# Gate and up by the Strassen identity over two levels, with token sums and h in DRAM

## The chip, the cores and the metric

The kernel runs on one core of one Trainium2 chip. The metric is the device time in microseconds of one execution. The profile gives the span from the first to the last instruction of one profiled execution, and the time of that execution beside it.

## What is computed

The input x is (8, 256, 1024) in fp32: 2048 tokens of 1024 features. Four layers follow, each added to its input, each with LoRA adapters of rank 16 that are picked for each of the eight batch entries by four index vectors.

```python
# L0: a linear layer with bias and LoRA, 1024 -> 1024
x = x + (einsum('bti,oi->bto', x, W) + b + ((x @ A[id]) @ B[id]) * 2)
# L1: a gated MLP, 1024 -> 2752 -> 1024, LoRA (scale 0.5) on gate, up and down
gate = lora_add(einsum('bnh,fh->bnf', x, W_gate), x, A_gate, B_gate)
up   = lora_add(einsum('bnh,fh->bnf', x, W_up),   x, A_up,   B_up)
act  = silu(gate) * up
x = x + lora_add(einsum('bnf,hf->bnh', act, W_down), act, A_down, B_down)
# L2, L3: LoRA alone
x = x + einsum('bnr,bor->bno', einsum('bni,bri->bnr', x, B2[id]), A2[id])
x = x + einsum('bnr,bor->bno', einsum('bni,bri->bnr', x, B3[id]), A3[id])
```

Everything stays in fp32.

## The kernel before

**Tiling.** On the chip x is transposed: features on the 128 partitions (8 chunks of 128, `NC`), tokens along the free dimension. The tokens are worked in two blocks (`NBLK`) of 1024, and each block is two halves (`NN`) of 512[...]. The hidden size 2752 is 21 chunks of 128 (`FC`) and a remainder of 64 (`FR`), in six groups: five of four chunks and one of the last chunk with the remainder.

**Products.** Every large product uses one level of the Strassen identity in Winograd's form, seven products for eight. The class `Job` writes one such product out: its weights as a 2 x 2 block matrix (two chunks of outputs by two halves of the inputs) against the tokens as a 2 x 2 block matrix (two halves of the inputs by two halves of the tokens). `weight_sums` (L244 to L247) makes the four sums of the weights on VectorE for each job, `token_sums` (L253 to L256) the four sums of the tokens once for each stage. `Job.run` fixes the order by hand: products 1, 5, 6, 3, then hooks (`middle`), then 7, 2, 4. `Job.block` (L274) issues one product: for gate and up four matmuls of 128x128 weights on 512 tokens, for down two (one in its last group). Products accumulate in the banks `pa`, `pb`, `pc`; ScalarE copies three intermediate states out (`early`, L328), VectorE adds (L306 and the adds in `done`).

**Gate and up.** One job is one chunk f: its output rows are gate chunk f and up chunk f, so 21 jobs a block (`gate_up`). After the products `lora` adds the LoRA parts with four matmuls of 32 rows (`expand`, L230), then `done` computes silu(gate) x up with ScalarE's sigmoid (L516) and VectorE. The remainder's 64 gate rows and 64 up rows are one ordinary product (`mixed`, L470, with L481 for its LoRA), and `shrink2` computes the LoRA inputs `tgu` through `shrink_into` (L206). x1 (the input of layer 1), its sums and h stay in SBUF, in a pool of 67 tiles of 128x512.

**Down.** When a group of gate and up is complete, `shrink_hidden` and `sum_hidden` run in the middle of the next group's first job, and four down jobs for that group follow. Their results add up in x2. The last group carries the remainder and down's LoRA as extra rows. `tables23`, `shrink23` and `last_layers` (L725) then do layers 2 and 3 and store the output.

**Order.** The list `jobs` is the order of all engines: block 0 with layer 0 (four jobs, the first one a `plain` product, L420, while x arrives), then `mixed`, then 21 gate-up jobs with the down jobs of group g - 1 after the first job of group g, then the last down jobs and `last_layers`; then block 1. SP's queue loads each job's weights one job ahead (`load_pair`, two times 512 KB; `following.loaded = following.load()`), and the following job's weight sums are issued before products 2 and 4 of this one. GpSimd only gathers LoRA tables (L176).

Of the kernel before, what the change touches and what calls it, by code (L numbers as in the profile page):

```python
# [7 lines left out]
F32 = mybir.dt.float32  # L8
# [10 lines left out]
R = 16  # L19
# [11 lines left out]
GROUPS = ((0, 4), (4, 8), (8, 12), (12, 16), (16, 20), (20, 21))  # L31


@with_exitstack
def kernel(
# [11 lines left out]
    wg: bass.AP,  # L47
    wu: bass.AP,
    wmix: bass.AP,
# [6 lines left out]
    bmix: bass.AP,  # L56
# [22 lines left out]

    nc = tc.nc  # L80

    const = ctx.enter_context(tc.tile_pool(name="const", bufs=1))
    xpool = ctx.enter_context(tc.tile_pool(name="x", bufs=67))
    wpool = ctx.enter_context(tc.tile_pool(name="w", bufs=5))
    swpool = ctx.enter_context(tc.tile_pool(name="sw", bufs=2))
    cpool = ctx.enter_context(tc.tile_pool(name="c", bufs=8))
# [4 lines left out]
    tpool = ctx.enter_context(tc.tile_pool(name="t", bufs=2))  # L91
    ps_a = ctx.enter_context(tc.tile_pool(name="ps_a", bufs=2, space=bass.MemoryType.PSUM))
    ps_b = ctx.enter_context(tc.tile_pool(name="ps_b", bufs=1, space=bass.MemoryType.PSUM))
    ps_c = ctx.enter_context(tc.tile_pool(name="ps_c", bufs=2, space=bass.MemoryType.PSUM))
    ps_l = ctx.enter_context(tc.tile_pool(name="ps_l", bufs=1, space=bass.MemoryType.PSUM))
    ps_t = ctx.enter_context(tc.tile_pool(name="ps_t", bufs=1, space=bass.MemoryType.PSUM))
    ps_d = ctx.enter_context(tc.tile_pool(name="ps_d", bufs=1, space=bass.MemoryType.PSUM))

    def xtile(name):
        return xpool.tile([P, 512], F32, tag="x", name=name)  # L100

    def ctile(name):
        return cpool.tile([P, 512], F32, tag="c", name=name)
# [38 lines left out]

    off_b = const.tile([P, 4, NBLK], I32, tag="off_b", name="off_b")
    off_gu = const.tile([P, NBLK], I32, tag="off_gu", name="off_gu")
    sel_v = sel.rearrange("p l (k n) -> p l k n", n=NN)
    for r in range(4):
        rows = slice(32 * r, 32 * r + 32)
        nc.vector.tensor_copy(off_b[rows], sel_v[rows, :, :, r // 2])
        nc.vector.tensor_copy(off_gu[rows], sel_v[rows, 1, :, r % 2])
    nc.vector.tensor_scalar(off_b, off_b, float(R), rank_f, op0=ALU.mult, op1=ALU.add)  # L150
    nc.vector.tensor_scalar(off_gu, off_gu, float(R), rank_f, op0=ALU.mult, op1=ALU.add)
    nc.vector.tensor_single_scalar(off_gu[64:], off_gu[64:], float(SLOTS1 * R), op=ALU.add)
# [19 lines left out]
    nc.scalar.dma_start(out=bias, in_=b0)  # L172

# [28 lines left out]
    def shrink_into(ps, r, a, chunks, c, n, src, start, stop):  # L202


        v = a.rearrange("p b (r c) -> p (b r) c", c=chunks)[:, 2 * n * R : 2 * (n + 1) * R, c]
        nc.tensor.matmul(ps[32 * r : 32 * r + 32, :], v, src, start=start, stop=stop)  # L206

    def shrink(a, src, scale, name):

        ps = ps_t.tile([P, 512], F32, tag="t", name=name)  # L210
        for c in range(HC):
            for r in range(4):
                k = (r % 2) * HC + c
                shrink_into(ps, r, a, NC, k, r // 2, src[k][r // 2], c == 0, c == HC - 1)
        return rank_out(ps, scale, f"{name}_s")

    def shrink2(a, b, src, scale, name):

        ps = ps_t.tile([P, 512], F32, tag="t", name=name)
        order = [0, 1, 2, 4, 5, 6, 3, 7]  # L220
        for c in order:
            for r in range(4):
                shrink_into(
                    ps, r, (a, b)[r // 2], NC, c, r % 2, src[c][r % 2], c == order[0], c == order[-1]
                )
        return rank_out(ps, scale, f"{name}_s")
# [11 lines left out]


    def weight_sums(a11, a12, a21, a22, width, name):  # L240

        s = swpool.tile([P, 3, 512], F32, tag="sw", name=name)
        s2, s3, s4 = (s[:, j, :width] for j in range(3))
        nc.vector.tensor_sub(s3, a11, a21)  # L244
        nc.vector.tensor_add(a21, a21, a22)
        nc.vector.tensor_sub(s2, a21, a11)
        nc.vector.tensor_sub(s4, a12, s2)  # L247
        return {1: a11, 2: a12, 3: s4, 4: a22, 5: a21, 6: s2, 7: s3}

    def token_sums(b11, b12, b21, b22, t1, name):  # L250

        t2, t3, t4 = (xtile(f"{name}_t{j}") for j in (2, 3, 4))
# [4 lines left out]
        return {1: b11, 2: b21, 3: b22, 4: t4, 5: t1, 6: t2, 7: t3}  # L257

    class Job:


        def __init__(self, name, load, sums, moving, lora, early, done):
            self.name, self.load, self.make, self.moving = name, load, sums, moving
            self.lora, self.early, self.done = lora, early, done
            self.before, self.middle, self.plain = [], [], None

        def sums(self):
            self.stationary = self.make(self.loaded)

        def block(self, ps, j, start=False):  # L270
            moving = self.moving()
            w = self.stationary[j]
            for k, m in enumerate(moving):
                nc.tensor.matmul(  # L274
                    ps,
                    w[:, k * P : (k + 1) * P],
                    m[j],
                    start=start and k == 0,
                    stop=k == len(moving) - 1,
                    skip_group_check=True,  # L280
                )

        def run(self, following):
            for hook in self.before:
                hook()
            if following:
                following.loaded = following.load()
            if self.plain:
                self.plain(self.loaded, lambda: [hook() for hook in self.middle])
                following.sums()  # L290
                return
            n = self.name
            pa = ps_a.tile([P, 512], F32, tag="a", name=f"pa_{n}")
            pc = ps_c.tile([P, 512], F32, tag="c", name=f"pc_{n}")
            s1, p5, s2 = (ctile(f"{j}_{n}") for j in ("s1", "p5", "s2"))
            self.block(pa, 1, start=True)
            self.early(1, s1, pa)
            self.block(pc, 5, start=True)
            self.early(5, p5, pc)
            self.block(pa, 6)  # L300
            self.early(6, s2, pa)
            self.block(pc, 3)
            for hook in self.middle:
                hook()
            self.block(pa, 7)
            nc.vector.tensor_add(p5, p5, pa)  # L306
            if following:
                following.sums()
            pb = ps_b.tile([P, 512], F32, tag="b", name=f"pb_{n}")
            self.block(pb, 2, start=True)  # L310
            self.block(pa, 4)
            pl = self.lora(pa, pb, pc) if self.lora else None
            self.done(s1, s2, p5, pa, pb, pc, pl)

    def by_halves(w):
        return [w[j][:, h : h + HC, :].rearrange("p c m -> p (c m)") for j in (0, 1) for h in (0, HC)]

    def load_pair(w, i, v, j, name):
        out = []
        for x, y in ((w, i), (v, j)):  # L320
            t = wpool.tile([P, NC, P], F32, tag="w", name=f"{name}_{len(out)}")
            nc.sync.dma_start(out=t, in_=x[y])
            out.append(t)
        return out

    def copy(dst, src, bias_=None):
        if bias_ is None:
            nc.scalar.activation(dst, src, AF.Identity)  # L328
        else:
            nc.scalar.activation(dst, src, AF.Identity, bias=bias_)  # L330

    jobs = []
    arrival = [c + h for c in range(HC) for h in (0, HC)]

    def block(blk):
        st = {}


        def load_x():
            st["x"] = xs = [[None] * NN for _ in range(NC)]  # L340
            for n in range(NN):
                for i, k in enumerate(arrival):
                    xs[k][n] = xtile(f"x_{blk}_{k}_{n}")
# [6 lines left out]
            st["xm"] = [  # L350
                token_sums(*xs[c], *xs[c + HC], xtile(f"x_{blk}_{c}_t1"), f"x_{blk}_{c}")
                for c in range(HC)
            ]

        st["x1"] = [[None] * NN for _ in range(NC)]
        st["x1m"] = [None] * HC

        def layer0(o):
            p = o + HC

            def early(j, dst, ps):
                b, x = {1: (o, (o, 0)), 5: (p, (p, 1)), 6: (o, (o, 1))}[j]
                copy(dst, ps, bias[:, b : b + 1])
                nc.vector.tensor_add(dst, dst, st["x"][x[0]][x[1]])

            def lora(pa, pb, pc):
                pl = ps_l.tile([P, 512], F32, tag="l", name=f"pl_0_{blk}_{o}")
                b, t = st["b0"], st["t0"]
                expand(pb, b, o, t, 0, 64)
                expand(pc, b, o, t, 64, 128)  # L370
                expand(pa, b, p, t, 0, 64)
                expand(pl, b, p, t, 64, 128, start=True)
                return pl
# [473 lines left out]
```

## Time and profile before

| what | value |
|---|---|
| median of 3 runs | 1947.23 us (1945.86 to 1947.27) |
| the profiled execution's own time | 1945.51 us |
| its span | 1943.7 us |
| granted TensorE clock | 0.999 |
| a gate-up job (starts at 170.28, 195.58, 220.88 us) | 25.30 us |
| VectorE add of two 128x512 tiles | 687 to 691 ns |
| ScalarE copy of a 128x512 bank (L328) | 597 ns |
| weight load of 512 KB, from issue to landing | 3.4 us |

In the profile PE is TensorE's matmuls, PEld its weight loads, DVE VectorE, ACT ScalarE, POOL GpSimd, SP the engine whose queue issues most transfers. A group row names line, engine, operation, destination and sources, the shapes and the number of records; then the busy time and the mean duration of one in ns, and the idle time of the engine just ahead of them with what ended it. A matmul record starts when the pass starts and its end is modelled, so records of neighbours overlap, and spacing is read from starts in the timeline.

### The profile page before, as it was taken

What the parts mean: (1) busy time and instruction counts of PE and PEld (TensorE: products, weight loads), DVE (VectorE), ACT (ScalarE), POOL (GpSimd) and SP (SyncE); (2) the same over time, 40 slices, a digit from 0 to 9 for tenths busy, and PEclk for the clock granted to TensorE, in tenths of its full rate; (3) what the DMA queues carried; (4) which work ended last, traced back from release to release, by engine and by line L of the source; (5) the groups of instructions that cost most, each with busy time, mean ns of one, the idle gap of its engine ahead of it and who ended that gap; (6) DMA issues with size and microseconds to landing.
All of it is one profiled execution on the core that took longest, in us unless ns stands there. A gap on an engine that the chain in (4) does not pass through costs nothing.

```text
span 1943.7 us, 13193 instructions
## 1 busy us (share of the span) xinstructions
PE 1925.8 (99%) x5140; PEld 820.6 (42%) x5140; DVE 809.9 (42%) x1370; ACT 263.1 (14%) x435; POOL 120.1 (6%) x137
## 2 busy tenths in 40 slices
PE   8999999999999999999999999999999999999998
PEld 3444444444444444444344444444444444444442
DVE  5332344254345236147734233432533442543466
ACT  0001111111111102012200011111111111111121
POOL 5001010010010010012110100000000100100000
PEclk9999999999999999999999999999999999999999
DMA  6111111111111111114231111111111101111102
GB/s 210 46 45 42 35 61 33 43 52 43 43 52 43 44 45 36 41 41 135 74 118 43 54 44 49 46 44 45 40 43 34 61 33 44 46 43 44 35 25 87
DMA packets 36622, 104.23 MB, mean 54 GB/s; under 512 B 6032, under 2 KB 7184, under 8 KB 36560
## 3 DMA queue, kind: packets, MB, share of 16 engines
q1 hardware_dynamic: 25216, 82.32, 13.1%
q0 software_dynamic: 4864, 10.56, 1.8%
q10 hardware_dynamic: 6480, 10.51, 1.6%
q8 instruction: 40, 0.66, 0.1%
q14 instruction: 22, 0.18, 0.0%
HBM read 94.98 MB, written 8.39 MB: 53 GB/s over the span
## 4 chain that ended last, share of the span: by engine, by line
PE 98%; DVE 1%; DMA 0%; issue 0%; ACT 0%; DVEq 0%; SPq 0%
PE pa L274 51%; PE pc L274 25%; PE pb L274 12%; PE pb L230 3%; PE pp L420 1%; PE pm L470 1%; PE td L206 1%; PE p L206 1%; PE tgu L206 1%; PE p L230 1%; DVE x L725 0%; PE t L206 0%; DMA x<-in_xT_dram 0%; PE pa L230 0%; PE pm L481 0%; DVE hr L579 0%
## 5 line engine op out<-in xcount | busy, mean ns | idle before, releaser
L274 PE MATMUL pa<-x_t,swgu 128*128 128x512 f32 x672 | 303.1, 594 | 0.0
L306 DVE TENSOR_TENSOR p<-p,pa 128x512 f32<-128x512 f32 x97 | 66.6, 687 | 522.0 <-PE pa L274 521.9
L274 PEld LDWEIGHTS pa<-x_t,swgu 128*128 128x128 f32 x672 | 126.9, 190 | 164.0 <-issue 164.0
L274 PE MATMUL pa<-h_t,swd 128*128 128x512 f32 x352 | 168.6, 597 | 0.0
L328 ACT ACTIVATE s<-pa 128x512 f32<-128x512 f32 x180 | 107.5, 597 | 385.8 <-PE pa L274 385.3
L274 PE MATMUL pa<-x,wgu 128*128 128x512 f32 x336 | 154.9, 603 | 0.0
L274 PE MATMUL pc<-x,swgu 128*128 128x512 f32 x336 | 151.1, 592 | 0.0
L274 PE MATMUL pc<-x_t,wgu 128*128 128x512 f32 x336 | 151.0, 592 | 0.0
L274 PE MATMUL pa<-x_t,wgu 128*128 128x512 f32 x336 | 151.0, 592 | 0.0
L274 PE MATMUL pb<-x,wgu 128*128 128x512 f32 x336 | 151.0, 592 | 0.0
L516 ACT ACTIVATE sg<-s 128x512 f32<-128x512 f32 x42 | 26.5, 630 | 659.5 <-DVE s L515 659.5
L274 PEld LDWEIGHTS pa<-h_t,swd 128*128 128x128 f32 x352 | 65.4, 190 | 87.8 <-issue 82.1
L274 PEld LDWEIGHTS pa<-x,wgu 128*128 128x128 f32 x336 | 61.0, 190 | 90.0 <-issue 90.0
L625 DVE TENSOR_TENSOR s<-s,x 128x512 f32<-128x512 f32 x96 | 66.3, 691 | 75.6 <-ACT s L328 75.4
L274 PEld LDWEIGHTS pa<-x_t,wgu 128*128 128x128 f32 x336 | 63.8, 190 | 80.4 <-issue 78.7
L274 PEld LDWEIGHTS pb<-x,wgu 128*128 128x128 f32 x336 | 63.8, 190 | 80.4 <-issue 80.4
L274 PEld LDWEIGHTS pc<-x,swgu 128*128 128x128 f32 x336 | 63.8, 190 | 80.4 <-issue 80.4
L274 PEld LDWEIGHTS pc<-x_t,wgu 128*128 128x128 f32 x336 | 63.8, 190 | 80.4 <-issue 80.4
L244 DVE TENSOR_TENSOR swgu<-wgu,wgu 128x512 f32<-128x512 f32 x42 | 28.9, 689 | 139.1 <-DMA wgu<-in_wu_dram 139.1
L274 PE MATMUL pa<-h,wd 128*128 128x512 f32 x176 | 84.4, 598 | 0.0
L274 PE MATMUL pc<-h,wd 128*128 128x512 f32 x176 | 83.4, 592 | 0.0
L176 POOL DMA_INDIRECT bgu<-in_bgu_dram,off_gu x12 | 11.4, 947 | 1105.3 <-PE pl L230 1104.7
(170 smaller groups left out, 2107.9 us busy)
## 6 DMA issues: line engine op xcount, KB each, us to landing
wgu<-in_wg_dram SPq DMA_DIRECT2D x42, 512.0 KB, 3.4
wgu<-in_wu_dram SPq DMA_DIRECT2D x42, 512.0 KB, 3.5
wd<-in_wd_dram SPq DMA_DIRECT2D x40, 512.0 KB, 3.4
w<-in_w_dram SPq DMA_DIRECT2D x16, 512.0 KB, 3.6
out_dram<-x ACTq DMA_DIRECT2D x32, 256.0 KB, 4.2
x<-in_xT_dram SPq DMA_DIRECT2D x24, 256.0 KB, 5.9
x<-in_xT_dram ACTq DMA_DIRECT2D x8, 256.0 KB, 6.4
wmix<-in_wmix_dram SPq DMA_DIRECT2D x2, 512.0 KB, 3.5
```

What stands on the lines that cost most here:

```text
L176: nc.gpsimd.indirect_dma_start(out=t, out_offset=None, in_=table, in_offset=bass.IndirectOffsetOnAxis(ap=off, axis=0),)
L206: nc.tensor.matmul(ps[32 * r : 32 * r + 32, :], v, src, start=start, stop=stop)
L230: nc.tensor.matmul(ps, b[lo:hi, i * P : (i + 1) * P], t[lo:hi, :], start=start, stop=True, skip_group_check=True,)
L244: nc.vector.tensor_sub(s3, a11, a21)
L274: nc.tensor.matmul(ps, w[:, k * P : (k + 1) * P], m[j], start=start and k == 0, stop=k == len(moving) - 1, skip_group_check=True,)
L306: nc.vector.tensor_add(p5, p5, pa)
L328: nc.scalar.activation(dst, src, AF.Identity)
L420: nc.tensor.matmul(pss[j, n], wt[:, c, :], x[c][n], start=i == 0, stop=i == NC - 1)
L470: nc.tensor.matmul(pss[n], w[:, c, :], x1[c][n], start=c == order[0], stop=c == order[-1], skip_group_check=True,)
L516: nc.scalar.activation(sg[0], s1, AF.Sigmoid)
L625: nc.vector.tensor_add(dst, dst, base(*{1: (o, 0), 5: (p, 1), 6: (o, 1)}[j]))
```

## The change

**Two levels.** For gate and up the outer level of the identity takes the weights as (gate, up) by (two halves of the inputs) and the tokens as (two halves of the inputs) by (two halves of the tokens). Each of its seven products is again split into seven. So 49 products stand where two full levels have 64, on quarters of 256 tokens. The class `Quads` does this for a group of four chunks (`nq` = 2, two pairs of chunks side by side in one bank). Its seven outer products are seven *units*, in the order 1, 2, 3, 5, 6, 7, 4; each unit runs seven blocks of `nq` x 2 matmuls of 128x128 weights on 256 tokens. The last block of a unit is put off to the middle of the next (`pending`, `flush`). X, E, Z, Y are four accumulators in SBUF; at the end of units 2, 6, 7, 4 one of them is a finished quarter of gate or up.

**Rest.** The last chunk, the remainder of 64 + 64 rows and the LoRA shrink (as 128 extra columns of the weights) make a group of their own with `nq` = 1 (`rest`), which runs first of a block's groups. It takes the place of `mixed`, `shrink2` and the tables `be` and `bm`.

**Weight sums.** `outer` and `inner_sums`, and the weight sums of down, are on GpSimd. Layer 0's stay on VectorE.

**Tokens.** The token sums of both levels are made once for each block, on VectorE, after layer 0 (`prepare_tokens`); layer 0 of both blocks now comes ahead of everything else. They are stored to DRAM (`toks`, 7 x 2 tiles of 128 x 1792), and each unit loads its two tiles of 917 KB (`load_tok`). x1 goes to DRAM (`x1d`) and is loaded for down as x2. h goes to DRAM for each group (`hd`), and down, which runs as a stage of its own after all groups of a block, loads it.

**Work beside.** `done` puts the finishing of a quarter (LoRA expand into a bank of its own, add, sigmoid, products, store, shrink for down) into the queue `beside`, from which each slot of a unit takes a share. SBUF is one pool of 22 tiles of 8 KB a partition; PSUM is 2 banks a, 1 b, 1 c and 4 l.

Layer 0's evictions add bias and x on VectorE straight from the bank; its order of outputs is 0, 2, 1, 3. A down eviction is one VectorE add into x2.

```diff
-    class Job:
-        def block(self, ps, j, start=False):
-            moving = self.moving()
-            w = self.stationary[j]
-            for k, m in enumerate(moving):
-                nc.tensor.matmul(ps, w[:, k * P : (k + 1) * P], m[j], ...)
...
-        first = gate_up(0, 0)
-        first.before.insert(0, mixed)
...
+    class Quads:
+            for s in range(len(ORDER)):
+                u = Unit(f"{name}_{s}", lambda at, s=s: self.step(s, at), share)
+                u.before(1, 0, lambda s=s: self.load_tok(s))
+                u.before(1, 1, lambda s=s: self.inner_sums(s))
+                self.units.append(u)
+            first = self.units[0]
+            first.before(3, 0, lambda: (self.load("B11"), self.load("B12")))
+            first.before(2, 0, lambda: self.load("B22"))
+            first.before(1, 0, lambda: self.load("B21"))
+            self.units[0].at(2, lambda: self.outer("T3", "B22", "B12", "sub"))
+            self.units[1].at(3, lambda: self.outer("B12", "B12", "B11", "sub"))
+            self.units[2].at(2, lambda: self.outer("B11", "T3", "B11", "add"))
+            self.units[4].at(2, lambda: self.outer("B21", "B21", "B11", "sub"))
...
+        def load_tok(self, s):
+            i = ORDER[s]
+            self.tok[i] = []
+            for kk in range(2):
+                t = big(f"tk_{self.name}_{s}_{kk}")[:, : 7 * S]
+                nc.sync.dma_start(out=t, in_=toks[self.blk][PLACE[i], kk])
+                self.tok[i].append(t)
...
+        def inner_sums(self, s):
...
+            nc.gpsimd.tensor_add(s1, m21, m22)
+            nc.gpsimd.tensor_sub(s2, s1, m11)
+            nc.gpsimd.tensor_sub(s3, m11, m21)
+            nc.gpsimd.tensor_sub(s4, m12, s2)
...
+            def block(ps, j, start=False):
+                for q in range(nq):
+                    for kk in range(2):
+                        nc.tensor.matmul(
+                            ps[:, q, :],
+                            w[j][:, q, kk * P : (kk + 1) * P],
+                            tok[kk][:, SLOT[j] * S : (SLOT[j] + 1) * S],
...
+            def first(r, k, ps):
+                if old is None:
+                    copy(view(out, r, k), ps)
+                else:
+                    nc.vector.tensor_add(view(out, r, k), view(old, r, k), ps)
+            def more(r, k, ps):
+                nc.vector.tensor_add(view(out, r, k), view(out, r, k), ps)
+                whole(r, k)
+            also = {5: ("Z", "Y"), 6: ("Z", "X"), 7: ("Y", "X")}.get(i)
+            def whole(r, k):
+                if also:
+                    a, b = (view(self.c[x], r, k) for x in also)
+                    nc.vector.tensor_add(a, a, b)
+            at(0)
+            pa = half(ps_a, "pa")
+            block(pa, 1, start=True)
+            first(0, 0, pa)
+            at(1)
+            pc = half(ps_c, "pc")
+            block(pc, 5, start=True)
+            first(1, 1, pc)
+            at(2)
+            flush()
+            at(3)
+            block(pa, 6)
+            first(0, 1, pa)
+            at(4)
+            block(pc, 3)
+            more(0, 1, pc)
+            at(5)
+            pb = half(ps_b, "pb")
+            block(pb, 2, start=True)
+            more(0, 0, pb)
+            at(6)
+            block(pa, 7)
+            more(1, 1, pa)
+            at(7)
+            def last():
+                block(pa, 4)
+                first(1, 0, pa)
+                whole(1, 0)
+                if i in self.ENDS:
+                    n, table, key = self.ENDS[i]
+                    self.done(n, table, self.c.pop(key))
+            pending.append(last)
...
+            def done(n, table, c):
+                beside.append((0, lora))
+                for r in range(4):
+                    beside.append(
+                        (0.69, lambda r=r: nc.vector.tensor_add(c[:, r], c[:, r], lo[r]))
+                    )
+                    if table == 0:
+                        beside.append(
+                            (0, lambda r=r: nc.scalar.activation(lo[r], c[:, r], AF.Sigmoid))
+                        )
...
+                if (n, 1 - table) in held:
+                    u, v = held[n, 1], held[n, 0]
+                    for r in range(4):
+                        beside.append(
+                            (0.69, lambda r=r: nc.vector.tensor_mul(u[:, r], u[:, r], v[:, r]))
+                        )
+                    def store():
+                        nc.sync.dma_start(out=hd[blk][g, n], in_=u.rearrange("p r t -> p (r t)"))
+                        shrink_hidden(g, n, [u[:, r] for r in range(4)])
+                    beside.append((0.7, store))
...
+        rest()
+        for g in range(REST):
+            job(g)
...
+    for blk in range(NBLK):
+        layer0(blk)
+    for blk in range(NBLK):
+        gate_up(blk)
+        down_projection(blk)
...
+        def at(slot):
+            for f in hooks.pop((i, slot), ()):
+                f()
+            spent = 0
+            while beside and spent < u.share:
+                cost, f = beside.popleft()
+                f()
+                spent += cost
```

In the prediction, lines of the changed kernel are L386 for the matmuls of `block`, L418 for the add of `first`, L421 for that of `more`, L774 for the store of h. X, Z, Y, E, `whole` and u x v (the product of up and silu(gate)) are as above. A block is one inner product of the identity: A7 is inner product 7, into the bank `pa`. pd is the shrink of h for down's LoRA, td the sum that collects it.

## The prediction

> **What bounds the kernel now.** I read the busy line and the chain of waits first, because they tell whether removed work can be seen in the end.
>
> ```profile
> PE 1925.8 (99%) x5140; PEld 820.6 (42%) x5140; DVE 809.9 (42%) x1370; ACT 263.1 (14%) x435; POOL 120.1 (6%) x137
> DMA packets 36622, 104.23 MB, mean 54 GB/s; under 512 B 6032, under 2 KB 7184, under 8 KB 36560
> q1 hardware_dynamic: 25216, 82.32, 13.1%
> PE 98%; DVE 1%; DMA 0%; issue 0%; ACT 0%; DVEq 0%; SPq 0%
> ```
>
> TensorE works 99% of the span and is 98% of the chain: every product left out is time, until something else is late. VectorE has 58% left, GpSimd 94%. q1 moved 82.32 MB in 13.1% of 1943.7 us, so 323 GB/s when it runs.
>
> The timeline of TensorE gives the price of a product:
>
> ```profile
> 416.82 3.60 PE L274 MATMUL pb<-x,wgu 128*128 128x512 f32 x8
> 420.25 3.60 PE L274 MATMUL pa<-x_t,wgu 128*128 128x512 f32 x8
> ...
> 424.85 1.98 PE L274 MATMUL pa<-h,wd 128*128 128x512 f32 x4
> 426.67 1.88 PE L274 MATMUL pc<-h,wd 128*128 128x512 f32 x4
> ```
>
> The last column counts records; one fp32 matmul of the program makes two (passes). Four matmuls start 3.43 us apart (420.25 - 416.82), so one costs 0.857 us, a pass 429 ns. The group rows say 594 ns because records overlap; I use starts. The weight loads have records of their own:
>
> ```profile
> 424.85 0.30 PEld L274 LDWEIGHTS pa<-h,wd 128*128 128x128 f32 x2 [0.76 <-issue]
> 425.39 0.19 PEld L274 LDWEIGHTS pa<-h,wd 128*128 128x128 f32 x1 [0.24 <-issue]
> 899.57 1.09 PEld L676 LDWEIGHTS pba<-bb,a2s 128*32 128x32 f32 x32 [0.76 <-issue]
> 899.57 1.21 PE L676 MATMUL pba<-bb,a2s 128*32 128x32 f32 x32
> ```
>
> A load's record is 190 ns, under a 429 ns pass. Two queued loads started 0.11 us apart (0.30 - 0.19), and 32 loads of 32 columns with their passes took 1.2 us, 35 ns each.
>
> [...]
>
> **The change part by part.**
>
> *Products (removed).* Before: 42 gate-up jobs x 28 matmuls = 1176 x 0.857 = 1008 us; the remainder (L470) 13.93 us a block, 28; its LoRA (L481) 3; the shrink tgu 7.03 a block, 14. Together 1053. After: ten groups of 7 units x 7 blocks x 4 matmuls and two rest groups of half that are 2156 matmuls of 256 tokens. A pass of 512 took 429 ns[...], so 256 should take 215.6 ns and a matmul 0.431: 929 us. **Saved 124.** LoRA expands (42 sets of four before, 44 after, 1.15 us each), the shrinks for down, down and layer 0 keep their TensorE work.
>
> *Evictions and finishing in the ten groups (moved, finer).* A block is now 1.72 us and a bank comes back after 3.45 us. By unit 1, 2, 3, 5, 6, 7, 4 VectorE has 3, 7, 3, 7, 11, 11, 7 operations of 512 for evicting and adding: 49. Finishing adds 34 (LoRA adds, two products, td): 83 x 0.69 = 57 us beside 91 us of TensorE (196 x 0.431 + 4 x 1.15 + 1.9 for shrinks). On the sum it is hidden; in two places it isn't. In unit 7 the finishing of Z makes 20 operations, 13.8 us against 14.2, and block A7 needs the bank that an eviction queued behind these frees: by the order of operations TensorE waits 1.1 us. In the next group's first units the X chain (adds, sigmoid products, u x v and two evictions: 14 x 0.69 = 10 us after its expand) must end before the shrink pd, which TensorE reaches after 8.6 us: 1.6 us. That is 2.7 a group if nothing disturbs VectorE.
>
> *Weight sums on GpSimd (moved, and the unknown).* A group has 28 inner operations of 512 and 8 outer of 1024[...]. They are issued a unit ahead, so their length alone is hidden. But VectorE's 12 adds of `whole` and 8 of u x v have two SBUF inputs[...], just in the two tight places. Lower bound nothing; upper, every one of them waits for a whole inner operation there[...]. I take 5 with the 2.7: **+50 over ten groups (28 to 85).**
>
> *Tokens through DRAM (added).* In a group a unit loads two tiles of 917 KB in 12.07 us: with weights (4.2 MB a group) and h stores (2.1), (12.85 + 4.2 + 2.1) MB / 91 us = 210 GB/s. The rate that the engines give is seen in two stretches (us, busy of PE, PEld, DVE, ACT, POOL, clock, DMA share, GB/s):
>
> ```profile
> 16.00:20.00 4.00, 4.00 (x11) 1.82 (x10) 1.66 (x5) 1.28 (x1) 3.02 (x3) 1.00 1.00 342
> 975.00:985.00 10.00, 10.00 (x26) 4.31 (x24) 4.09 (x8) 1.37 (x2) 0.95 (x1) 1.00 0.98 331
> ```
>
> At 340 the groups are covered: by the order of buffers a token load may start 26 to 38 us before its product (the lead is that of the tile it replaces). In SP's queue it can stand behind a store of h (L774) that waits for the last u x v; that is late by the X chain's few us, less than the lead. The *rest groups* aren't: half the products (98 x 0.431 = 42 us) but the same 12.85 MB, 305 GB/s for these alone. In block 0 SP's queue also holds the stores of the second block's sums (half of 12.9 MB), x1 (2 MB) and the next group's weights (4.2): 25 MB / 0.34 = 74 us, and token loads stand in SP's order behind stores that wait for VectorE. Some of it runs before or after: a loss of 25. In block 1 the output stores (4.2 MB) share the rate and hold tiles that the loads need: 7, and 5 for the rest group's own chain (eight ScalarE copies, masks, expand, shrink), which nothing covers at its end. **+37 (25 to 55).**
>
> *Layer 0 and down.* Token sums (60 us of VectorE, all told) are spread over layer 0's slots and the x1 stores follow; layer 0's weight sums stay on VectorE. x1 and h come back through SP, 16.8 and 42 MB both ways, under down's 264 us a block (308 matmuls x 0.857); down's sums go to GpSimd (four of 256[...], a unit of 12 us). I take **+5 (0 to 10)** for layer 0's slots where VectorE is full, nothing for down: its TensorE covers it.
>
> *Sum.* The profiled execution took 1945.51 us: 1945.5 - 124 + 50 + 37 + 5 = 1913.5. The median lies 1.7 above it: **1915**. Low end of all terms: 1945.5 - 124 + 28 + 25 = 1875; high end 1945.5 - 124 + 85 + 55 + 10 = 1971.
>
> **Rivals.**
>
> *Everything is covered.* VectorE keeps ahead since GpSimd and it rarely meet, and the transfers run as the rate allows. For: VectorE's 63% and DMA's 60% inside a group. Against: the two tight places come from the order alone. About 28 + 12 of stalls: 1887; with none of either, 1860.
>
> *A 256-token pass doesn't hide its weight load (slower).* Each pass loads 128 columns anew, and the load's record of 190 ns is now nearly as long as the pass of 216. If load and exchange bind at x ns, the cost is 4312 passes x (x - 215.6): at 240 ns, 105 us, so 2020. It turns the sign from 215.6 + 32/4312 us = 223 ns. For: no pass of 256 with a load of 128 is in this trace. Against: loads 0.11 us apart, 35 ns for a load of 32 columns. So the record seems to hold latency that overlaps. Chance 0.08.
>
> *VectorE and GpSimd lock each other (slower).* Same place as the +50, price beyond 8.2 us a group: each two-input operation waits for a GpSimd one, evictions come late, and TensorE idles at A7 and pd. At 10 us a group, 1965. Chance 0.09 to be past 8.2.
>
> *Transfers bind (little or no gain).* If small pieces or SP's order cut the rate to 210 GB/s, each ordinary group waits too; at 190 it loses some 9 us, 1960. Against: 331 to 342 seen with loads of whole rows; token rows are 7 KB. Chance 0.05.
>
> *That it doesn't do what it says* can't be: the instruction lists have the 2156 matmuls and the loads.
>
> **How the numbers follow.** The forecast (1890 to 1940) has 0.58, the covered case 0.20, the three slower ones 0.22 together, a part of which ends within the bound. What a measurement can tell from no change is about 0.2%, 1943.3 to 1951.1: faster 0.78, same 0.05, slower 0.17. The range for 8 in 10 leaves out the deepest covered case and the far side of the slower ones: 1868 to 1960.
>
> **What would show it.** Right: starts of a block of four matmuls of 256 every 1.72 us; TensorE busy near 1802 (1925.8 - 124) of 1912 with idle time released by VectorE's evictions (L418, L421) and by DMA at the first units of each rest group; VectorE some 1050 us, GpSimd some 800, 340 MB moved. A block of 1.9 us or more shows the weight load binding; idle TensorE after DMA inside ordinary groups shows the transfers; VectorE's adds with two SBUF inputs far above 0.69 us show the lock. I am wrong if the pitch differs from 1.72 us, or if the idle time of TensorE isn't some 90 us, in these two places.

## The result and the profile after

The changed kernel took 1921.36 us (median; 1920.13 to 1929.02) against 1946.85 us of the kernel before: a ratio of 0.9878, 95% interval [0.9852, 0.9904]. Forecast were 1915 us and 1868 to 1960. The profiled execution was the slowest of its four, 1929.02 us with a span of 1927.3 us.

The page of the changed kernel, its busy line and the DMA lines:

```profile
PE 1865.9 (97%) x6916; PEld 1188.0 (62%) x6916; DVE 1135.8 (59%) x1656; ACT 171.9 (9%) x294; POOL 935.5 (49%) x773
DMA packets 71722, 343.48 MB, mean 178 GB/s; under 512 B 10065, under 2 KB 11217, under 8 KB 59345
q1 hardware_dynamic: 59680, 320.89, 45.3%
```

TensorE is still busy 97%, but of a shorter sum; VectorE has 326 us more (1136; some 1050 were forecast), GpSimd 815 more (936; some 800, my estimate, since the trace of before has no sum on GpSimd), and 343 MB were moved (340). Busy time hides what matters here, since a matmul record's end is modelled: 1866 is not 1802, though no product got longer. The timeline of TensorE in one group of four chunks shows the pitch and the first stall (start us, us, what, idle before it):

```profile
522.23 1.89 PE L386 MATMUL pb<-tk,w_B 128*128 128x256 f32 x8
523.96 1.89 PE L386 MATMUL pa<-tk,sw 128*128 128x256 f32 x8
525.68 1.89 PE L386 MATMUL pa<-tk,w_B 128*128 128x256 f32 x8
528.18 4.08 PE L227 MATMUL pd<-c_Y,ad 128*32 128x512 f32 x8 [0.60 <-DVE c_Y L774]
532.19 1.99 PE L386 MATMUL pc<-tk,sw 128*128 128x256 f32 x8
```

A block of four matmuls starts 1.73 us after the last (523.96 - 522.23): 216 ns a pass of 256 tokens, as forecast. The weight load of 190 ns is hidden, and the rival that it wouldn't be is out. The shrink pd holds TensorE for 4.01 us (532.19 - 528.18); elsewhere the same eight passes take 1.03.

VectorE in the same stretch, and then GpSimd:

```profile
521.92 1.88 DVE L767 TENSOR_TENSOR c_X<-c_X,pl 128x512 f32<-128x512 f32 x3
523.71 4.41 DVE L774 TENSOR_TENSOR c_Y<-c_Y,c_X 128x512 f32<-128x512 f32 x1
528.05 0.68 DVE L774 TENSOR_TENSOR c_Y<-c_Y,c_X 128x512 f32<-128x512 f32 x1
528.65 0.68 DVE L421 TENSOR_TENSOR c_X<-c_X,pc 128x512 f32<-128x512 f32 x1
```

```profile
523.85 1.28 POOL L364 TENSOR_TENSOR sw<-w_B 128x512 f32<-128x512 f32 x1
525.08 1.27 POOL L366 TENSOR_TENSOR sw<-w_B 128x512 f32<-128x512 f32 x1
526.30 1.27 POOL L365 TENSOR_TENSOR sw<-sw,w_B 128x512 f32<-128x512 f32 x1
```

Three products with one operand in PSUM (L767) take 1.88 us, 0.60 apart. L774 is the line of u x v (the store of h is at L778), which reads two tiles of SBUF. The first of the two is on record from 523.71 us, just ahead of GpSimd's sums, and ends at 528.12, after all three of them: 4.41 us, the longest of its row. The second takes 0.68.

The second place is the start of block 0's rest group. VectorE first, then TensorE:

```profile
241.56 1.41 DVE L490 TENSOR_TENSOR sa<-x 128x1024 f32<-128x1024 f32 x1
243.00 1.63 DVE L491 TENSOR_TENSOR sa<-sa,x 128x1024 f32<-128x1024 f32 x1
244.56 4.04 DVE L492 TENSOR_TENSOR sb<-x,x 128x1024 f32<-128x1024 f32 x1
248.52 4.03 DVE L493 TENSOR_TENSOR sb<-x,sa 128x1024 f32<-128x1024 f32 x1
...
253.08 0.41 DVE L421 TENSOR_TENSOR c_r_X<-c_r_X,pc_r 128x256 f32<-128x256 f32 x1
```

```profile
245.03 1.03 PE L386 MATMUL pa_r<-tk_r,w_r_B 128*128 128x256 f32 x4
253.63 2.04 PE L386 MATMUL pc_r<-tk_r,sw_r 128*128 128x256 f32 x4 [7.58 <-DVE c_r_X L421]
255.47 1.92 PE L386 MATMUL pb_r<-tk_r,w_r_B 128*128 128x256 f32 x4
```

The last token sums of block 1 stand in VectorE's order ahead of the eviction at 253.08. Two of them take 4.04 us instead of 1.22, and TensorE idles 7.58 us. After that a block of two matmuls takes 1.84 us (255.47 - 253.63), not 0.86: TensorE is granted half its clock for 10.2 us, from 248.6 to 258.8, of which the last 5.2 fall on work. Before the last microseconds of the span this trace has five stretches of half clock, of 3.4, 6.8 or 10.2 us. They follow stalls of 2.0 us and more, and none follows those of 1.3.

Of TensorE's waits in this stage, these are the longest and those for token loads (us in total, times, longest):

```profile
PE pc_r L386 <- DVE c_r_X L421: 7.6, 1, 7.6
PE pa_r L386 <- DMA tk_r<-toks: 2.6, 1, 2.6
PE pa_r L386 <- DVE tt_h L508: 1.9, 1, 1.9
```

The last is put down to a token sum, `tt_h`, which no product of the stage reads. It is the wait for a load: the one that SP issued at 263.07 us, behind stores of the sums, landed at 271.29, and the product started at 271.43.

Where the time went, by stages. Nominal is the sum of the passes at 216 or 429 ns and of the small sets as they run undisturbed; "again" is the changed kernel profiled a second time, at 1920.04 us, near its median:

| stage, us | nominal | first profile | again |
|---|---|---|---|
| layer 0, both blocks | 219.3 (kernel before) | 230.9 | 231.8 |
| rest group, block 0, to the first undisturbed part of group 0 | 61.4 | 94.2 | 85.0 |
| ordinary groups, block 0 | 447.6 | 475.7 | 475.2 |
| rest group, block 1 | 72.5 | 76.4 | 76.5 |
| ordinary groups, block 1 | 448.1 | 473.2 | 472.9 |

### The profile page after: what moved, and what is told of

It is laid out like the page before. It is cut to its first block, busy times and chain, and to the rows that moved or that the text cites. A ratio compares the mean times of both kernels' runs of the same rounds, so it can differ in the third digit from the quotient of the medians.

```text
span 1927.3 us, 18519 instructions
## 1 busy us (share of the span) xinstructions
PE 1865.9 (97%) x6916; PEld 1188.0 (62%) x6916; DVE 1135.8 (59%) x1656; ACT 171.9 (9%) x294; POOL 935.5 (49%) x773
## 5 line engine op out<-in xcount | busy, mean ns | idle before, releaser
L386 PE MATMUL pa<-tk,sw 128*128 128x256 f32 x1120 | 270.8, 385 | 13.3 <-DVE c_X L418 13.3
L386 PE MATMUL pc<-tk,sw 128*128 128x256 f32 x1120 | 265.7, 380 | 0.0
L386 PEld LDWEIGHTS pa<-tk,sw 128*128 128x128 f32 x1120 | 208.6, 190 | 76.6 <-issue 22.9
L297 PE MATMUL pa<-ht,wd 128*128 128x512 f32 x512 | 236.3, 594 | 0.5 <-DVE x L963 0.4
L386 PEld LDWEIGHTS pc<-tk,sw 128*128 128x128 f32 x1120 | 212.5, 190 | 36.1 <-issue 8.1
L386 PE MATMUL pa<-tk,w_B 128*128 128x256 f32 x960 | 229.7, 382 | 0.0
L963 DVE TENSOR_TENSOR x<-x,pa 128x512 f32<-128x512 f32 x192 | 131.6, 686 | 138.6 <-PE pa L297 138.5
L386 PEld LDWEIGHTS pa<-tk,w_B 128*128 128x128 f32 x960 | 182.0, 191 | 36.8 <-issue 13.2
L364 POOL TENSOR_TENSOR sw<-w_B 128x512 f32<-128x512 f32 x60 | 76.2, 1271 | 209.7 <-PE pa L386 121.1
L386 PE MATMUL pb<-tk,w_B 128*128 128x256 f32 x480 | 113.8, 380 | 0.0
L386 PEld LDWEIGHTS pb<-tk,w_B 128*128 128x128 f32 x480 | 91.3, 190 | 13.7 <-issue 1.7
L418 DVE TENSOR_TENSOR c_X<-c_X,pa 128x512 f32<-128x512 f32 x90 | 61.5, 683 | 62.5 <-PE pa L386 62.3
L366 POOL TENSOR_TENSOR sw<-w_B 128x512 f32<-128x512 f32 x60 | 85.2, 1420 | 0.0
```

Source lines behind the costliest of these rows:

```text
L297: nc.tensor.matmul(ps, w[j][:, k * P : (k + 1) * P], m[j], start=start and k == 0, stop=k == len(moving) - 1, skip_group_check=True,)
L364: nc.gpsimd.tensor_add(s1, m21, m22)
L366: nc.gpsimd.tensor_sub(s3, m11, m21)
L386: nc.tensor.matmul(ps[:, q, :], w[j][:, q, kk * P : (kk + 1) * P], tok[kk][:, SLOT[j] * S : (SLOT[j] + 1) * S], start=start and q == 0 and ...
L418: nc.vector.tensor_add(view(out, r, k), view(old, r, k), ps)
L963: nc.vector.tensor_add(x2[k][j], x2[k][j], ps)
```

## The experiments

Theories: the **lock** (VectorE operations with two SBUF inputs wait for GpSimd's), the **order** (VectorE's chain is too long ahead of pd and A7 by itself), and **transfers** (the rest group is bound by its token loads). Each kernel is timed against the kernel before on its chip. In the first four below, all on one chip, layer 0's first shrink took 14 to 16 us where it takes 3.6 in the runs on other chips, so I compare those four by stages.

**No weight sums on GpSimd.** `inner_sums` and `outer` left out:

```diff
-            nc.gpsimd.tensor_add(s1, m21, m22)
...
-            self.sums[i] = {1: m11, 2: m12, 3: s4, 4: m22, 5: s1, 6: s2, 7: s3}
+            self.sums[i] = {1: m11, 2: m12, 3: m12, 4: m22, 5: m21, 6: m22, 7: m11}
```

> This kernel leaves out GpSimd's weight sums of gate and up (inner and outer); the products use raw weight blocks in their place, everything else is as in the changed kernel. Lock theory (VectorE operations with two SBUF inputs wait for GpSimd's): VectorE's u x v and whole adds all take 0.69 us, the token sums of 1024 take 1.22; the stall at pd falls from 3.84 us a group to about 1.6, that at A7 from 1.57 to about 1.1, and the first stall of the rest group of block 0 from 7.9 us to about 2.5, with less of the half clock after it. Sum: 8 x 2.7 + 5 + 10, so about 35 us less than the changed kernel, near 1885. Order theory (the chain of VectorE operations alone is too long): groups stay at 97.3 us each and the total within 8 us of the changed kernel's 1921.

1886.97 us, ratio 0.9679 [0.9662, 0.9696]. The ordinary groups took 454.0 and 454.4 us, one group 92.2 instead of 97.4; no stall over 0.7 us is left in them, at pd or A7. So the lock theory holds, and more than I gave it: nothing is left for the order. That the total is near the 1885 expected is chance: the groups gave 40 us where 22 were expected, the rest group some 5 where 15 were, and layer 0's shrink took 11 more. In the rest group TensorE's first stall on VectorE fell from 7.6 to 1.1 us, but the stage only to 81.2 us (86.4 in the next kernel, on the same chip), as TensorE's waits there show (us in total, times, longest):

```profile
PE pa_r L382 <- DMA tk_r<-toks: 10.1, 3, 4.4
PE pc_r L382 <- DVE c_r_X L417: 1.1, 1, 1.1
```

With the lock gone, loads of tokens are late: they stand in SP's queue behind the stores of the same sums, and the DMA engines have no pause (the columns are those of the prediction: us, busy of PE, PEld, DVE, ACT, POOL, clock, DMA share, GB/s):

```profile
255.00:295.00 40.00, 28.41 (x108) 21.95 (x106) 19.29 (x40) 3.23 (x9) 1.28 (x4) 0.87 1.02 415
```

So the transfer theory is not out for this stage: transfers are the next limit, right behind the lock.

**u x v with one operand in PSUM.**

```diff
-nc.vector.tensor_mul(c[:, r], c[:, r], lo[r])
+nc.vector.tensor_mul(lo[r] if second else c[:, r], c[:, r], lo[r])
-nc.vector.tensor_mul(u[:, r], u[:, r], v[:, r])
+nc.vector.tensor_mul(u[:, r], lo[r], (v if table == 1 else u)[:, r])
```

(and the LoRA add of up into `lo[r]` likewise)

> The last operation ahead of u x v writes its result into the PSUM bank of the LoRA part, so that u x v has one SBUF input and one PSUM input; the number and order of VectorE's operations is unchanged. Lock theory: no u x v above 0.75 us (4.4 us was seen), the stall at pd falls from 3.84 to about 1.6 us a group, and the kernel gains 8 x 2.2 = 18 us, near 1903; A7's stall changes by less than 0.5. Order theory: within 4 us of the changed kernel.

1896.16 us, ratio 0.974 [0.971, 0.9769]. Groups 454.2 and 454.5 us: the whole of the gain that leaving GpSimd's sums out gave in the groups. VectorE in the stretch that answers to the one above (L787 is u x v here), and GpSimd beside it:

```profile
521.24 0.68 DVE L787 TENSOR_TENSOR c_Y<-pl,c_Y 128x512 f32<-128x512 f32 x1
521.84 0.68 DVE L421 TENSOR_TENSOR c_X<-c_X,pc 128x512 f32<-128x512 f32 x1
522.43 1.28 DVE L787 TENSOR_TENSOR c_Y<-pl,c_Y 128x512 f32<-128x512 f32 x2
```

```profile
521.39 1.28 POOL L364 TENSOR_TENSOR sw<-w_B 128x512 f32<-128x512 f32 x1
522.62 1.26 POOL L366 TENSOR_TENSOR sw<-w_B 128x512 f32<-128x512 f32 x1
```

Both engines run at their own pace at the same time. The number and order of operations is as it was, so the stall was the lock on eight operations a group. A7's stall went too (1.6 us in all are left of 13), where I expected it to stay.

**pd three slots later.**

```diff
+                        for _ in range(3):
+                            beside.append((0.85, lambda: None))
-                        shrink_hidden(g, n, [u[:, r] for r in range(4)])
+                        beside.append((0.7, lambda: shrink_hidden(g, n, ...)))
```

> The four shrink matmuls pd are put three slots later on TensorE; nothing else is moved. If pd's stall is only its early place in TensorE's order (behind u x v), all of its 3.84 us in each of 8 groups goes: about -30 us, near 1891, lock or not. If VectorE as a whole is late there (a backlog), the wait comes back at the next evictions (first, more) and less than 10 us is gained.

1942.68 us, ratio 0.9965 [0.9953, 0.9977]. Nothing gained: groups 479.1 and 474.6 us, 6 more than in the changed kernel. pd waits no longer, the next eviction does:

```profile
PE pc L386 <- DVE c_X L421: 20.7, 7, 3.0
PE pa L386 <- DVE c_X L418: 10.4, 8, 1.3
```

u x v still took up to 4.4 us, and an eviction stands behind it; the idle time is now in one piece of 3 us, and five of these seven stalls are followed by 3.4 us of half clock. pd's early place was not the cause.

**Block 1's second token sums put off to group 1.**

```diff
-                u.at(8, lambda kk=o % 2: finished(kk))
+                if blk == 1 and i == 3:
+                    deferred.append(lambda kk=o % 2: finished(kk))
...
+            if blk == 0 and g == 1:
+                q.units[0].at(6, deferred.pop())
```

> The second half of block 1's token sums and its stores, which stood ahead of the first evictions of the rest group of block 0, are put off to the second group of block 0. VectorE theory for the rest group (sums ahead of evictions, slowed by GpSimd, then half clock after the idle time): the stretch from the rest group's start to the first LoRA-free part of group 0, 94.2 us in the changed kernel against 61.4 of plain TensorE work, falls to about 70, and no half clock is granted there; total about -22 us, near 1899. Transfer theory (tokens at 305 GB/s for the rest group bind): the stretch stays above 82 us, since the token loads remain, with waits on DMA tk_r. Costs elsewhere by the deferred sums: up to 5 us in group 1.

1929.26 us, ratio 0.9901 [0.9882, 0.9919]: no gain in all. The rest stage fell to 67.3 us without half clock, but the groups of block 0 grew to 488.1. TensorE's waits in group 1, and the sums there:

```profile
PE pc L387 <- DVE c_Z L422: 7.2, 1, 7.2
PE pc L387 <- DVE c_E L422: 2.5, 1, 2.5
```

```profile
427.73 6.24 DVE L509 TENSOR_TENSOR tt_h<-x 128x512 f32<-128x512 f32 x2
433.89 0.67 DVE L422 TENSOR_TENSOR c_E<-c_E,pc 128x512 f32<-128x512 f32 x1
```

The first of these two sums took 5.63 us, the second 0.68; GpSimd made two sums of 1024 meanwhile (4.66 us together). The loss follows the sums to wherever GpSimd works. As the stores were put off with the sums, this run doesn't part the share that VectorE had in the rest stage from that of the transfers.

**The changed kernel again**, as the measure for what follows.

> The changed kernel again, unaltered, as the measure for the runs beside it: a ratio to the kernel before of 0.985 to 0.991, as at first. In the four kernels measured since, the shrink of layer 0's first block took 14 to 16 us where it took 3.6 in the first profile; if that belongs to the chip or the run and not to those kernels, it is here too, some 11 us of it.

1921.17 us, ratio 0.9882 [0.9861, 0.9902]; the shrink took 3.60 us. It took 3.60 as well in the versions below that hold the edits of the first two kernels, on other chips, so that its 14 to 16 was not these edits'. What it was is not shown.

**Sums of x earlier in layer 0.**

```diff
-                    u.at(1, lambda c=c: sum_x(c))
+                    u.at(0, lambda c=c: sum_x(c))
```

> The token sums of x for block 0 are put ahead of the first job's evictions on VectorE, where x arrives and VectorE is idle. If layer 0's stall (4.1 us ahead of a product of the second job, then half clock) is VectorE's queue order, it goes: layer 0 becomes 5 to 8 us shorter and the kernel 0.3 to 0.4% faster than the unaltered one. Rival (the weights of that job land late): the stall stays.

1911.48 us, ratio 0.9819 [0.9803, 0.9836]: 9.7 us less, where 5 to 8 were expected. The rest group starts at 231.4 us instead of 240.7. What is gone is this wait of the unaltered kernel on the second job's weight sums, which stood behind 16 sums of x on VectorE:

```profile
PE pc L297 <- DVE w L284: 3.9, 1, 3.9
```

**Block 1's second token sums in block 0's down stage**, from x1 loaded again from DRAM.

```diff
-            prepare_tokens(blk, kk, [st["x1", n, kk] for n in range(NN)])
+            if blk == 1 and kk == 1:
+                deferred.append(reload)
...
+                    if blk == 0 and g == 1:
+                        u.at(5, lambda: deferred.pop()())
```

> The second half of block 1's token sums is made in block 0's down stage, from x1 loaded again from DRAM. Theory (the same sums collide with GpSimd's wherever GpSimd is busy, and with the rest group's loads): in down GpSimd works a quarter of the time, so that the rest group's stretch falls from 94 us to about 67 as when they were put into group 1, but the loss doesn't come back: 24 to 28 us less than the unaltered kernel. Rival (VectorE has no room for them without a stall on TensorE anywhere): down gets longer by more than 8 us.

1905.98 us, ratio 0.9794 [0.9778, 0.981]: 15 us less than the unaltered kernel, and down no longer (274.7 us to the next rest group, as before). The stage fell to 71.1 us. The 24 to 28 that I expected were reckoned from the first profile's 94.2, which held more half clock than the 85.0 of the run beside this one.

**The three together.**

> Three changes together: u x v with one input in PSUM, x sums early, second half of block 1's token sums in down. If the three losses are independent: groups 8 x 5.2 = 42 us, rest group 27, layer 0 5 to 8, so some 72 us less than the unaltered kernel, a ratio of 0.950 to 0.955 to the kernel before. If they share a cause, less than 60 us.

1858.23 us, ratio 0.9548 [0.9532, 0.9564], 63 us less than the changed kernel, where some 72 were expected. The parts add: layer 0 8.7, rest group 14.7, groups 21.3 and 18.6, 63.3 by stages; the rest group gave less than its 27. No half clock is left but at the end, and TensorE is busy 99%:

```profile
PE 1827.5 (99%) x6916; PEld 1176.2 (63%) x6916; DVE 1087.7 (59%) x1656; ACT 172.2 (9%) x294; POOL 920.1 (50%) x773
```

**The three together, half of the rest groups' token loads**, and **the three together without weight sums**:

```diff
+                if kk and self.nq == 1:
+                    self.tok[i].append(self.tok[i][0])
+                    break
```

> On the version with all three changes, the two rest groups load only one of the two token tiles of a unit and use it twice, so half of their 12.85 MB (the other half of the sums is left out of the products). Rest stages there were 70.3 and 76.4 us. Transfer theory as in the prediction (the rest group is bound by its token loads): both shrink by 5 us or more. If VectorE and the rest group's own chain set the remaining 9 us: less than 3 us.

> The version with all three changes, without GpSimd's weight sums of gate and up (raw weight blocks in their place). VectorE's whole adds still take up to 1.0 us on average there, 0.69 without a wait. If what is left of the lock costs TensorE nothing: the two stretches of ordinary groups (453.9 and 454.3 us) and the rest stages change by less than 3 us each. If the lock still costs: 10 us or more in all.

One execution of each: 1859.83 and 1847.31 us. With half the loads the rest stages were 72.2 and 78.4 us, no shorter than 70.3 and 76.4, at a DMA share of 0.69 where it was 0.85 and 0.81. TensorE waited 1.8 us in each on the group's own chain (`trep`), and half clock came in, three stretches of 3.4 us in the first stage and one in the second. Each costs at most 1.7 us, so that 67.1 and 76.7 would be left without them. With the sums and their stores moved, transfers thus set at most some 3 us of the first stage and none of the second. Without weight sums the groups were 453.2 and 453.2 (453.9 and 454.3), the rest stages 65.7 and 74.6: under 3 us but in one place, where 4.6 of the 9 us above nominal are still the lock's.

## Why the prediction was right, and where its steps were not

The total was right within 7 us, the sign and the range too; by the parts, that is luck. By the prediction's own steps, with the sizes of the second profile:

- **Products: held.** The pitch is 216 ns, about half of the 429 ns of a pass of 512. With the 124 us and the four measured terms below the sum is 1945.5 - 124 + 52 + 24 + 4 + 12.5 = 1914 us, against 1920; the 6 us between are in no term. The 215.6 ns of the prediction were my estimate, half of the 429 and 1 ns more. The load of 128 columns has a record of 190 ns here too, and the pitch shows nothing of it.
- **Ordinary groups: 52 us above nominal, forecast 50; the parts were wrong.** I took 27 us for the order and 23 for the lock. Measured: 40 for the lock (948.1 - 908.1 us of groups, with and without u x v's second SBUF input) and 12 that no stall owns, some 0.1 us at each change between products, expands and shrinks. The order costs nothing. Its step failed at one mis-sized term: I added VectorE's operations at their duration, 0.69 us, but back to back they start 0.60 us apart. The X chain's 14 then are 8.4 us, not 10, just under TensorE's 8.6, and the 20 of unit 7 are 12.0. (The 10 - 8.6 of the prediction is also 1.4, not 1.6.)
- **The lock per group: I took 2.3; it was 4.0 as a mean of ten, 5.2 where both stalls stand.** The step that failed is that an operation waits for one GpSimd operation. In the trace one waiting u x v stayed out through three in a row, 4.41 us, each of them a whole sum of 1.27 or 1.28 us. The 5 us that I put on a group, 2.7 of them the order's, and the upper end of 85 were my estimate: the trace of before has no GpSimd sum that a VectorE operation could meet. The rival with the lock needed 8.2 a group and came to 6.4 with what the switches cost.
- **Rest groups: 24 and 4 us above nominal (33 and 4 in the first profile), forecast 25 and 12; the mechanism of the first was wrong.** I had put the 25 on token loads. These do stand behind stores in SP's queue, as forecast, but TensorE waited for them only 4.5 us in all. Its longest stall, 7.6 us, was on an eviction behind token sums on VectorE that GpSimd shut out (4.04 us each; 1.22 in the kernel without its weight sums), for which the sum had nothing. In the first profile it cost some 10, as half of the 5.2 us at half clock behind it is lost too; half clock was not in the sum either, 10.2 us of it in that stage in the second profile and 27 in the first. The rate that I took was too low, 340 GB/s where 415 were seen. Still the transfers are close: without GpSimd's sums the stage stayed 20 us above nominal, with 10.1 us of waits for token loads. Putting half of the sums off, with their stores, gave 14 us; how much of it is VectorE's and how much the stores' no run separates.
- **Layer 0: 12.5 us, forecast 5 (0 to 10).** I had named its full VectorE slots but not the place: 16 sums of x ahead of the second job's weight sums; putting them first gave 9.3 back, the half clock after it included.
- **Down: nothing, as forecast** within some 3 us. Its weight sums of 256 on GpSimd took 0.73 us in the median.
- **The covered rival was priced wrongly.** 1945.5 - 124 + 28 + 12 is 1861.5, and 1821.5 without any stall, not 1887 and 1860.

So the order, put at 27 us, cost nothing; token loads, put at 25, made TensorE wait 4.5; the lock, put at 23, was 40 and reached into the rest group too; and the half clock was missing. The sum came out near by errors of both signs.

## What to carry to other kernels

When work is moved to GpSimd, count not its length but the VectorE operations with two SBUF inputs that meet it (a u x v took up to 4.42 us beside GpSimd's sums, 0.68 without a wait), above all those that stand ahead of a PSUM eviction; letting one operand of u x v stay in PSUM (0.68 us each beside the same sums) took 40 us out of the groups at no cost. Add up a chain of VectorE operations by the spacing of their starts (0.60 us here), not by their durations (0.68). Price a stall of TensorE with the half clock that follows it: here 3.4 to 10.2 us of it behind most stalls of 2.0 us and more.

## What the runs showed of the hardware that I had not expected

- An operation of VectorE that waits for GpSimd is not next in turn: one u x v stayed out for three GpSimd sums of 1.27 us (4.41 us in all), one token sum of 512 for two of 2.33 (5.63).
- GpSimd's sums of 512 took 1.27 us in the clear, those of 1024 2.36, and the first up to 1.73 where they began beside a VectorE operation with two SBUF inputs. A group's come to 28 x 1.27 + 8 x 2.36 = 54 us, beside its 97.
- Between DRAM and SBUF 415 GB/s ran for 40 us (the kernel without weight sums); the trace of before shows 342 at 16 to 20 us and 388 at 20 to 26.
- Single stalls of TensorE of up to 1.8 us left the clock whole (1.4 and 1.8 in the version with all three changes, whose mean clock is 0.999), but for one of 1.4. Those of 2.0 to 7.6 us were followed by 3.4 to 10.2 us of half clock in most places, but not two of the seven of 3.0 us with pd late, nor one of 2.3 us in the version with all three changes. With half of the token loads two stretches followed no stall, only eight LoRA expands (`plr`, 3 us). Which stalls are caught differs from run to run: this makes some 7 of the 9 us between the rest stages of the two profiles of the changed kernel; a wait of 3.4 us against 0.4 on VectorE (`hr`) makes most of the rest.
